# The last batch's down product in seven half-size products instead of eight

## The chip, the cores and the metric

The kernel runs on one core of a Trainium2 chip. A core has a matrix engine (PE, TensorE), a vector engine (DVE, VectorE), a scalar engine (ACT, ScalarE), a general engine (POOL, GpSimd) and a queue that issues transfers (SP, SyncE). Each engine works through its own list of instructions strictly in order, and waits at an instruction whose inputs, or whose room for the output, another engine has not yet released. The metric is the device time of one execution in microseconds (us), the median over several runs.

## The reference

The input is 8 batches of 512 rows of 512 numbers, all in 32-bit floats. Every row goes through an attention layer and then through a feed-forward layer; both are wrapped in the same way:

```
x = x + layernorm(attention(layernorm(x)))
x = x + layernorm(ffn(layernorm(x)))
```

The feed-forward layer, cut to what matters here:

```
x_up   = x @ W_up.T   * scale_up            # 512 -> 2048
x_gate = x @ W_gate.T * scale_gate
h = silu(x_gate) * x_up
h = hadamard(h * SU_dp) / 64                # folded into the weights by the kernel
y = h @ W_down.T * (Wscale_dp * 64)         # 2048 -> 512: the "down product"
```

For one batch the down product multiplies a 512 x 2048 matrix by a 2048 x 512 matrix and scales column j of the result by `Wscale_dp[j]`. After it comes the layer norm over each row of 512 numbers (mean and variance of the row), and the residual `x` is added.

## The kernel before, in words

The kernel first runs the attention of all batches, then the feed-forward layer. The feed-forward layer takes batches two at a time; the up and gate products of a pair are themselves computed by Strassen's scheme (`deep`, L1123 to L1144: small 128x256 products `d`, with sums on DVE, ACT and POOL around them). Each finished block of `h`, 128 of the 2048 inner values by 512 rows, is called `g` (written by DVE at L1160) and kept on chip. There are NI = 16 blocks per batch. Between the small products PE is given parts of the down product of earlier batches (`down_parts`, L1225): for a block `g` and each of the four groups of 128 rows (t = 0..3) one matrix product into the accumulator `psy` of that group, 512 columns wide. In 32-bit floats PE runs every matrix product as two passes, so the profile counts two MATMUL records for each.

At the end of a batch `finish` (L1245) empties the four accumulators: DVE multiplies by the output scale `wsdp_bc` (L1250), takes mean and variance (`bn`, L99 and L100), POOL makes the inverse deviation (`inverse_std`, L104 and L105), DVE the shift (`shift_of`, L114 for four groups at once or L112 for one), ACT applies both (L1272), POOL adds the residual (L1275) and SP sends the rows out (L1276). These steps are put off in a list `ends` and are taken from it by `proceed`.

The change concerns the last part of the program, the lines from `b = NB - 1` on. At that point batch 6 still lacks its last three blocks (12 products), and the whole down product of batch 7 is to be done. The 16 blocks of weights for batch 7 lie on chip in four tiles `wd_home` (names `xb` and `wdl` in the trace); the last eight of them are loaded by SP just before (L1093). The order is written out by hand:

- `down_rows` on group 0 of batch 7, inner blocks 0 to 13 (14 products, L1516),
- the 12 remaining products of batch 6 (`down`), then all of `ends` for batch 6 (`proceed`),
- inner blocks 14 and 15 of group 0, then loads of the four residual tiles (L1544),
- for each further group its 16 products first, and then `end_rows` of the group before it. `end_rows` is: DVE scale (L1522), mean and variance (L99, L100), POOL inverse deviation (L104, L105), DVE shift (L112), ACT (L1527), residual add on POOL, or for the last group on DVE (L1528), and the output transfer (L1529).

The accumulators of this part come from `ubank`, a pool of four PSUM banks used in turn: the fifth tile that is asked for can be written only when the first has been read. Side tiles come from `pr_tile` (six of two rows of 512).

Of the kernel before, what the change touches and what calls it, by code (L numbers as in the profile page):

```python
# [10 lines left out]
F32 = mybir.dt.float32  # L11
BF16 = mybir.dt.bfloat16
I32 = mybir.dt.int32
AF = mybir.ActivationFunctionType
ALU = mybir.AluOpType
AX = mybir.AxisListType

P = 128
# [3 lines left out]
NT = S // P  # L22
INTER = 2048
NI = INTER // P
# [9 lines left out]
def sandwich_kernel(  # L34
# [19 lines left out]
    nc = tc.nc  # L54
# [6 lines left out]
    stat = ctx.enter_context(tc.tile_pool(name="stat", bufs=12))  # L61
# [13 lines left out]
    wsdp_bc = const.tile([P, D], F32, name="wsdp_bc")  # L75
# [21 lines left out]
    def bn(dst, src, name):  # L97
        st = stat.tile([P, 6], F32, tag="st", name=f"st_{name}")
        nc.vector.bn_stats(out=st, in_=src)  # L99
        nc.vector.bn_aggr(out=dst, in_=st)  # L100

    def inverse_std(mv, n, name):
        rs = stat.tile([P, NT], F32, tag="rs", name=f"rs_{name}")
        nc.gpsimd.tensor_add(rs[:, :n], mv[:, :n, 1], eps[:, :n])  # L104
        nc.gpsimd.tensor_tensor(rs[:, :n], rs[:, :n], nhalf[:, :n], ALU.pow)  # L105
        return rs

    def shift_of(mv, rs, n, name):

        sh = stat.tile([P, NT], F32, tag="sh", name=f"sh_{name}")  # L110
        if n == 1:
            nc.vector.tensor_scalar(sh[:, 0:1], mv[:, 0, 0:1], rs[:, 0:1], -1.0, ALU.mult, ALU.mult)  # L112
            return sh
        nc.vector.scalar_tensor_tensor(  # L114
            sh[:, :n], mv[:, :n, 0], -1.0, rs[:, :n], ALU.mult, ALU.mult
        )
        return sh
# [4 lines left out]
    NH = NI // 2  # L122
# [31 lines left out]
    rows = [(b, t) for b in range(NB) for t in range(NT)]  # L154
    room = {}
    xrow, xflat, xb = {}, {}, {}
# [63 lines left out]
    ops, home = {}, []  # L220
# [21 lines left out]
    with ExitStack() as actx:  # L242
# [474 lines left out]
        for t in range(NT):  # L717
            xn[0, t] = row.tile([P, D], F32, tag="xn", name=f"xn_0_{t}", bufs=3)
            rs, sh = norm0[t]
# [139 lines left out]
        for t in range(NG * NT):  # L859
            n, c = divmod(t, NT)  # L860
            b, i = divmod(t, NK * NT)
# [73 lines left out]
        b = NB - 1  # L935
# [24 lines left out]
        for qc in range(NT):  # L960
            y, rs, sh = ys.pop((b, qc))
# [16 lines left out]
    def ubank(name):  # L978
        return ps_u.tile([P, S], F32, tag="u", name=name)
# [8 lines left out]
    HS = S // 2  # L988
# [8 lines left out]
    def pr_tile(name):  # L997
        return fs.tile([P, 2, S], F32, tag="pr", name=name, bufs=6)
# [72 lines left out]
    def order_of(b):  # L1071
        return [f for i in range(NH) for f in ((i, i + NH) if b % 2 == 0 else (i + NH, i))]
# [10 lines left out]
    wd_last = []  # L1083
# [11 lines left out]
    wd_home = []  # L1095
# [53 lines left out]
    waiting = {b: [] for b in range(NB)}  # L1149
# [136 lines left out]
    def proceed(by=None):  # L1286
        if ends and by in (None, ends[0][0]):
            ends.pop(0)[1]()
# [3 lines left out]
    def part():  # L1292
        if not queue:
            queue.extend(down_parts())
        if queue:
            queue.pop(0)()
# [210 lines left out]
        scale(b, f, c[:, 1], c[:, 0])  # L1507


    b = NB - 1  # L1510
    blocks = [g for _, g, _, _ in waiting[b]]
    assert order_of(b) == [f for f, _, _, _ in waiting[b]]

    def down_rows(ps, t, lo, hi):
        for n in range(lo, hi):
            nc.tensor.matmul(  # L1516
                ps, lhsT=blocks[n][:, ts(t, P)], rhs=wd_last[n], start=n == 0, stop=n == NI - 1
            )

    def end_rows(ps, t, eng):  # L1520
        y = pr_tile(f"fy_{b}_{t}")[:, 0]
        nc.vector.tensor_mul(y, ps, wsdp_bc)  # L1522
        mv = stat.tile([P, NT, 2], F32, tag="mvf", name=f"mvz_{t}")
        bn(mv[:, 0, :], y, f"z{t}")
        rs = inverse_std(mv, 1, f"z{t}")
        sh = shift_of(mv, rs, 1, f"z{t}")
        nc.scalar.activation(y, y, AF.Identity, bias=sh[:, 0:1], scale=rs[:, 0:1])  # L1527
        eng.tensor_add(y, rest[t], y)  # L1528
        nc.sync.dma_start(out=out[b, ts(t, P), :], in_=y)  # L1529

    now[0] += 2
    while queue:
        part()
    ps = ubank("psz_0")
    down_rows(ps, 0, 0, NI - 2)
    while turn_of[0] < b:
        down()
    while ends:
        proceed()
    down_rows(ps, 0, NI - 2, NI)  # L1540
    rest = []
    for t in range(NT):
        rest.append(fs.tile([P, D], F32, tag="sig", name=f"xres_{b}_{t}", bufs=4))
        nc.sync.dma_start(out=rest[t], in_=x1d[b][ts(t, P), :])  # L1544
    for t in range(NT):
        if t + 1 < NT:
            following = ubank(f"psz_{t + 1}")
            down_rows(following, t + 1, 0, NI)
        end_rows(ps, t, nc.vector if t == NT - 1 else nc.gpsimd)
        ps = following  # L1550


def _rope_table():
# [61 lines left out]
```

## Time and profile before

| | us |
|---|---|
| median of 3 runs | 2101.75 (2101.75, 2101.75, 2103.98) |
| the profiled execution's own time | 2102.66 |
| its span, first to last instruction | 2100.9 |
| PE busy over the span | 2076.8 (99%) |
| POOL busy over the span | 1575.4 (75%) |
| DVE busy over the span | 1414.4 (67%) |
| ACT busy over the span | 745.3 (35%) |
| granted TensorE clock, mean over the span | 0.999 |

In the profile `out<-in` names what an instruction writes and reads, with buffer numbers left out; all times are us from the start of the span unless they are durations. An `x16` behind a row says that it merges 16 records of the same kind. PE records overlap (a pass ends after the next has begun), so the pace is read from starts. `PEld` is the load of a product's left operand, which runs beside PE. In brackets stands the idle time before an instruction and what ended it. The page has no line on the distance between the profiled execution's own time (2102.66) and the span (2100.9): 1.8 us lie outside the first and last instruction.

### The profile page before, as it was taken

What the parts mean: (1) busy time and instruction counts of PE and PEld (TensorE: products, weight loads), DVE (VectorE), ACT (ScalarE), POOL (GpSimd) and SP (SyncE); (2) the same over time, 40 slices, a digit from 0 to 9 for tenths busy, and PEclk for the clock granted to TensorE, in tenths of its full rate; (3) what the DMA queues carried; (4) which work ended last, traced back from release to release, by engine and by line L of the source; (5) the groups of instructions that cost most, each with busy time, mean ns of one, the idle gap of its engine ahead of it and who ended that gap; (6) DMA issues with size and microseconds to landing.
All of it is one profiled execution on the core that took longest, in us unless ns stands there. A gap on an engine that the chain in (4) does not pass through costs nothing.

```text
span 2100.9 us, 26741 instructions
## 1 busy us (share of the span) xinstructions
PE 2076.8 (99%) x9035; PEld 1057.4 (50%) x9042; DVE 1414.4 (67%) x2356; ACT 745.3 (35%) x1199; POOL 1575.4 (75%) x1629
## 2 busy tenths in 40 slices
PE   8999999999999999999999999999999999999998
PEld 4333333333333333344444677676676766777753
DVE  5698777676767677465545866678866678656542
ACT  3554545555555545522121122222222222222211
POOL 4787979787878889645453678788888879787852
PEclk9999999999999999999999999999999999999999
DMA  3112121212121122237454444444343344444432
GB/s 122 37 31 51 42 54 49 47 51 52 46 57 46 32 66 72 70 104 221 145 166 152 146 143 148 133 138 149 130 157 131 131 137 144 138 158 136 138 112 70
DMA packets 215913, 218.12 MB, mean 104 GB/s; under 512 B 87376, under 2 KB 147920, under 8 KB 215776
## 3 DMA queue, kind: packets, MB, share of 16 engines
q1 hardware_dynamic: 215424, 215.32, 33.2%
q8 instruction: 72, 1.18, 0.2%
q0 software_dynamic: 352, 1.08, 0.1%
q14 instruction: 65, 0.53, 0.1%
HBM read 169.18 MB, written 46.92 MB: 103 GB/s over the span
## 4 chain that ended last, share of the span: by engine, by line
PE 94%; DVE 3%; issue 1%; POOL 1%; ACT 1%; DMA 0%; SPq 0%; POOLq 0%; DVEq 0%; ACTq 0%
PE d L1123 24%; PE psy L1225 18%; PE s L527 6%; PE ops L606 6%; PE ps_k L439 5%; PE ps_y L662 5%; PE t L573 5%; PE u L1106 5%; PE g L1106 4%; PE psz L1516 3%; PE t L564 3%; PE l L623 2%; PE ps_q L454 2%; PE ps_v L466 1%; PE ps_cq L407 1%; PE fxh L207 1%
## 5 line engine op out<-in xcount | busy, mean ns | idle before, releaser
L1225 PE MATMUL psy<-wd,g 128*128 128x512 f32 x896 | 448.9, 592 | 0.0
L535 DVE TENSOR_REDUCE nm<-s 128x2 f32<-128x1024 f32 x256 | 300.8, 1216 | 175.1 <-PE s L527 175.1
L1347 POOL TENSOR_TENSOR pr<-pr,pr 128x512 f32<-128x512 f32 x294 | 391.6, 1357 | 9.0
L594 POOL TENSOR_TENSOR p<-p,p 128x512 f32<-128x512 f32 x244 | 330.2, 1384 | 22.1 <-PE ops L606 22.1
L585 ACT ACTIVATE p<-t 128x1024 f32<-128x1024 f32 x256 | 251.8, 1023 | 89.0 <-PE t L573 89.0
L1123 PE MATMUL d<-xb,wq 128*128 128x256 f32 x992 | 254.2, 380 | 1.9 <-DVE inner L1139 1.4
L1123 PEld LDWEIGHTS d<-tt,wq 128*128 128x128 f32 x864 | 164.0, 190 | 144.4 <-issue 106.0
L1123 PE MATMUL d<-tt,wq 128*128 128x256 f32 x864 | 233.8, 379 | 0.2 <-DVE pr L1144 0.2
L1140 POOL TENSOR_TENSOR pr<-inner 128x256 f32<-128x256 f32 x168 | 126.0, 750 | 138.5 <-DVE inner L1139 105.9
L1123 PEld LDWEIGHTS d<-xb,wq 128*128 128x128 f32 x992 | 186.7, 190 | 62.4 <-issue 30.1
L1225 PEld LDWEIGHTS psy<-wd,g 128*128 128x128 f32 x896 | 169.7, 190 | 49.3 <-issue 29.4
L1136 ACT COPY inner<-d 128x256 f32<-128x256 f32 x168 | 62.6, 373 | 309.6 <-PE d L1123 291.5
L1132 ACT COPY inner<-d 128x256 f32<-128x256 f32 x168 | 62.6, 372 | 300.3 <-PE d L1123 193.2
L527 PE MATMUL s<-kT,qT 32*128 32x512 f32 x1024 | 153.8, 639 | 0.7 <-DVE nm L535 0.7
L573 PE MATMUL t<-qT,kT 32*128 32x512 f32 x1024 | 142.8, 598 | 0.0
L606 PE MATMUL ops<-p,v 128*32 128x512 f32 x1024 | 136.8, 605 | 0.0
L1142 POOL TENSOR_TENSOR pr<-pr,inner 128x256 f32<-128x256 f32 x168 | 136.5, 813 | 0.0
L1123 PE MATMUL d<-T,wq 128*128 128x256 f32 x496 | 127.6, 380 | 0.2
L1144 DVE TENSOR_TENSOR pr<-d,inner 128x256 f32<-128x256 f32 x168 | 70.5, 420 | 75.5 <-PE d L1123 72.9
L439 PE MATMUL ps_k<-xT,wkr_sb 128*128 128x512 f32 x256 | 118.3, 605 | 0.7 <-ACT xT L397 0.7
L662 PE MATMUL ps_y<-wo_sb,oT 128*128 128x512 f32 x256 | 115.8, 593 | 0.9 <-DVE oT L657 0.6
L1135 DVE TENSOR_TENSOR inner<-d,inner 128x256 f32<-128x256 f32 x168 | 70.5, 419 | 62.4 <-PE d L1123 62.0
(219 smaller groups left out, 3263.8 us busy)
## 6 DMA issues: line engine op xcount, KB each, us to landing
wq<-wdeep SPq DMA_DIRECT2D x168, 448.0 KB, 4.2
wd<-wdd SPq DMA_DIRECT2D x112, 256.0 KB, 2.8
wdeep<-w SPq DMA_DIRECT2D x32, 448.0 KB, 5.5
xr<-in_x SPq DMA_DIRECT2D x32, 256.0 KB, 2.8
xin<-x1d SPq DMA_DIRECT2D x32, 256.0 KB, 4.0
xres<-x1d SPq DMA_DIRECT2D x32, 256.0 KB, 3.3
out<-fy SPq DMA_DIRECT2D x32, 256.0 KB, 2.0
rec<-rd SPq DMA_DIRECT2D x124, 64.0 KB, 2.0
```

Of the source, the lines that this page charges most:

```text
L439: nc.tensor.matmul(ps, lhsT=wkr_sb[:, k, ts(g, P)], rhs=xT[b][:, k, :], start=(k == 0), stop=(k == NK - 1),)
L527: nc.tensor.matmul(sp[j // 2][:, j % 2, :], lhsT=qT[b][rows, g, ts(qc, P)], rhs=kT[b][rows, g, :], start=True, stop=True,)
L535: nc.vector.tensor_reduce(nms[n][:, qc, 2 * h : 2 * h + 2], sp[h], AX.X, ALU.max, negate=True)
L573: nc.tensor.matmul(sp[j // 2][:, j % 2, :], lhsT=kT[b][rows, g, ts(c, P)], rhs=qT[b][rows, g, :], start=False, stop=True,)
L585: nc.scalar.activation(pt[n, c, h], sp[h], AF.Exp)
L594: nc.gpsimd.tensor_add(into, into, pt[n, c, j // 2][:, j % 2, :])
L606: nc.tensor.matmul(o_ps[n][j * DH : (j + 1) * DH, :], lhsT=vv[b][:, c, ds(g * P + j * DH, DH)], rhs=pt[n, c, j // 2][:, j % 2, :], start=( ...
L662: nc.tensor.matmul(ps, lhsT=oT[b][:, k, ts(qc, P)], rhs=wo_sb[:, k, :], start=False, stop=(k == NK - 1),)
L1106: nc.tensor.matmul(ps, lhsT=w[:, SLOT[n], k, :], rhs=rhs[:, k, :], start=k == 0, stop=k == 1)
L1123: nc.tensor.matmul(ps, lhsT=w[:, INNER[m]], rhs=rhs[m], start=True, stop=True)
L1225: nc.tensor.matmul(ys_[t], lhsT=g[:, ts(t, P)], rhs=w, start=n == 0, stop=n == NI - 1)
L1347: nc.gpsimd.tensor_add(pr[n][:, h], pr[a][:, h], pr[b][:, h])
```

## The change

The down product of batch 7 is cut into halves in all three directions: rows (256 + 256), inner values (blocks 0 to 7 and 8 to 15) and columns (256 + 256). Strassen's scheme in Winograd's form gets the four result quarters from seven products of halves instead of eight, with sums of operands before the products and sums of results after them. A product of halves is 2 groups of 128 rows x 8 inner blocks = 16 matrix products that are 256 columns wide.

- Products 1, 2 and 4 have one PSUM bank for each group of 128 rows; products 5, 6, 7 and 3 have both groups in one bank.
- `sums_of(5)`, `(6)`, `(7)`, `(3)` make sums of `g` blocks on POOL (8 instructions of 128x256 each); `sums_of(5)`, `(6)`, `(7)`, `(4)` make sums of weights on DVE (4 instructions of 128x512 each). `sums_of(3)` and `(4)` also multiply the output scale into weights on DVE (8 instructions of 128x256 each).
- The first half of products 1 and 2 stands where the 14 products of group 0 stood; their second half comes after the 12 products of batch 6.
- `sums_of(5)`, `(6)` and `(7)` are issued ahead of the remaining products and the `ends` of batch 6, so they stand ahead of these on DVE's and POOL's lists. The copies of product 1 (`m1`) stand behind the `ends` on ACT's list.
- The sums of the results go over ACT (copies), DVE and POOL; the output scale is put in where the terms lie.
- Each output row of 512 is closed in two parts: statistics of its left and right 256 columns are taken apart and aggregated; DVE multiplies by the inverse deviation and adds the residual in one instruction, ACT adds the shift, and each half goes out in a transfer of its own (8 instead of 4).

The engines' lists change only behind this point: PE gets 112 products 256 wide in place of 64 products 512 wide, POOL 52 instructions in place of 17, DVE 76 in place of 30, ACT 15 in place of 8, SP 8 output transfers in place of 4 (all counted from the first instruction after the last `g` block).

The diff, cut to its core:

```diff
-    def down_rows(ps, t, lo, hi):
-        for n in range(lo, hi):
-            nc.tensor.matmul(
-                ps, lhsT=blocks[n][:, ts(t, P)], rhs=wd_last[n], start=n == 0, stop=n == NI - 1
-            )
...
     now[0] += 2
     while queue:
         part()
-    ps = ubank("psz_0")
-    down_rows(ps, 0, 0, NI - 2)
...
+    def sums_of(n):
+        if n in (5, 6, 7, 3):
+            for i in range(NH):
+                if n == 5:
+                    nc.gpsimd.tensor_add(sum1[:, i], A[7](i), A[4](i))
+                elif n == 6:
+                    nc.gpsimd.tensor_sub(sum2[:, i], sum1[:, i], A[1](i))
+                elif n == 7:
+                    nc.gpsimd.tensor_sub(A[7](i), A[1](i), A[7](i))
+                else:
+                    nc.gpsimd.tensor_sub(A[3](i), A[2](i), sum2[:, i])
+        for j in range(NT):
...
+            if n == 5:
+                nc.vector.tensor_sub(ws1[:, two], b12, b11)
+            elif n == 6:
+                nc.vector.tensor_sub(ws2[:, two], b22, ws1[:, two])
+            elif n == 7:
+                nc.vector.tensor_sub(b12, b22, b12)
+            elif n == 3:
+                for i in range(2):
+                    nc.vector.tensor_mul(b22[:, i], b22[:, i], wsdp_bc[:, HS:])
+            elif n == 4:
+                nc.vector.tensor_sub(b21, b21, ws2[:, two])
+                for i in range(2):
+                    nc.vector.tensor_mul(b21[:, i], b21[:, i], wsdp_bc[:, :HS])
...
+    def last_product(n, rows=(0, 1), lo=0, hi=NH):
+        for r in rows:
+            if (n, r) not in acc:
+                ps = ubank(f"psz_{n}_{r}").rearrange("p (r s) -> p r s", r=2)
+                if n in (1, 2, 4):
+                    acc[n, r] = ps[:, 0]
+                else:
+                    acc[n] = ps
+                    acc[n, 0], acc[n, 1] = ps[:, 0], ps[:, 1]
+            for i in range(lo, hi):
+                nc.tensor.matmul(
+                    acc[n, r], lhsT=A[n](i)[:, ts(r, P)], rhs=W[n](i), start=i == 0, stop=i == NH - 1
+                )
...
+    for n in (1, 2):
+        last_product(n, hi=NH // 2)
+    for n in (5, 6, 7):
+        sums_of(n)
     while turn_of[0] < b:
         down()
     while ends:
         proceed()
-    down_rows(ps, 0, NI - 2, NI)
+    for n in (1, 2):
+        last_product(n, lo=NH // 2)
...
+    def close_rows(t):
+        h, r = divmod(t, 2)
+        mv, rs = of_rows.pop(t)
+        sh = shift_of(mv, rs, 1, f"z{t}")
+        for half in (left, right):
+            cols = ts(half is right, HS)
+            o = half[h][:, r]
+            nc.vector.scalar_tensor_tensor(o, o, rs[:, 0:1], rest[t][:, cols], ALU.mult, ALU.add)
+            nc.scalar.activation(o, o, AF.Identity, bias=sh[:, 0:1])
+            nc.sync.dma_start(out=out[b, ts(t, P), cols], in_=o)
+
+    for r in range(2):
+        nc.scalar.copy(m1[:, r], acc[1, r])
+        nc.vector.tensor_add(left[0][:, r], acc[2, r], m1[:, r])
+    for r in range(2):
+        nc.vector.tensor_mul(left[0][:, r], left[0][:, r], wsdp_bc[:, :HS])
+        rows_stats(r, 0, left[0][:, r])
+    last_product(5)
+    nc.scalar.copy(m5, acc[5])
+    sums_of(3)
+    last_product(6)
+    nc.vector.tensor_add(u2, acc[6], m1)
+    nc.gpsimd.tensor_add(v, u2, m5)
+    for r in range(2):
+        nc.gpsimd.tensor_mul(v[:, r], v[:, r], wsdp_bc[:, HS:])
+    sums_of(4)
+    last_product(7)
+    nc.vector.tensor_add(u3, acc[7], u2)
+    nc.gpsimd.tensor_add(right[1], u3, m5)
+    for r in range(2):
+        nc.vector.tensor_mul(u3w[:, r], u3[:, r], wsdp_bc[:, :HS])
+        nc.gpsimd.tensor_mul(right[1][:, r], right[1][:, r], wsdp_bc[:, HS:])
+        rows_stats(r + 2, 1, right[1][:, r])
+    last_product(3)
+    nc.vector.tensor_add(right[0], acc[3], v)
+    for t in range(2):
+        rows_stats(t, 1, right[0][:, t])
+        head_rows(t)
+    for t in range(2):
+        close_rows(t)
+    for r in range(2):
+        last_product(4, rows=(r,))
+        nc.vector.tensor_add(left[1][:, r], acc[4, r], u3w[:, r])
+        rows_stats(r + 2, 0, left[1][:, r])
+        head_rows(r + 2)
+    for r in range(2):
+        close_rows(r + 2)
```

## The prediction

> **What bounds the kernel now.** I read the page's first part, then the chain of waits over the last 75 us (the change touches nothing before 2027 us), then the timeline there, then the granted clock by stretches.
>
> ```profile
> PE 2076.8 (99%) x9035; PEld 1057.4 (50%) x9042; DVE 1414.4 (67%) x2356; ACT 745.3 (35%) x1199; POOL 1575.4 (75%) x1629
> ```
>
> ```profile
> 2024.07 1.73 PE d L1123 x8
> ...
> 2027.94 12.02 PE psz L1516 x28
> 2039.96 10.30 PE psy L1225 x24
> 2050.26 42.93 PE psz L1516 x100
> 2093.19 0.02 issue
> 2093.21 0.70 DVE fy L1522
> ```
>
> PE is busy 99%, and from 2027.94 to 2093.19 the chain holds nothing but PE: 152 passes without a gap. After its last pass come 7.71 us of closing work to the span's end (2100.9 - 2093.19). A 512-column pass is paced at 42.93/100 = 0.4293 us, a 256-column pass at 1.73/8 = 0.2158.
>
> The timeline shows what waits cost the engines that the change loads (start, duration, instruction):
>
> ```profile
> 1946.16 0.73 POOL L1140 TENSOR_TENSOR pr<-inner 128x256 f32<-128x256 f32 x1 [0.47 <-DVE inner L1139]
> 1946.85 0.73 POOL L1142 TENSOR_TENSOR pr<-pr,inner 128x256 f32<-128x256 f32 x1
> ...
> 2027.46 2.85 DVE L1160 SCALAR_TENSOR_TENSOR g<-pr,wsu 128x512 f32<-128x512 f32 x2
> ...
> 2028.58 1.19 POOL L1140 TENSOR_TENSOR pr<-inner 128x256 f32<-128x256 f32 x1
> ...
> 2029.73 1.17 POOL L1142 TENSOR_TENSOR pr<-pr,inner 128x256 f32<-128x256 f32 x1
> ...
> 2030.97 2.49 POOL L1347 TENSOR_TENSOR pr<-pr,pr 128x512 f32<-128x512 f32 x2
> ...
> 2033.50 0.75 DVE L1160 SCALAR_TENSOR_TENSOR g<-pr,wsu 128x512 f32<-128x512 f32 x1 [3.19 <-POOL pr L1347]
> ...
> 2054.55 1.02 POOL L105 TENSOR_TENSOR rs_o<-rs_o,nhalf 128x4 f32<-128x4 f32 x1
> ...
> 2055.80 2.93 ACT L1272 ACTIVATE fy<-fy,sh_o,rs_o 128x512 f32<-128x512 f32 x4 [22.81 <-DVE sh_o L114]
> ```
>
> A 128x256 sum on POOL takes 0.73 and follows the one before after 0.69 when DVE is quiet. When DVE runs an operation with two inputs from SBUF beside it, both slow down: POOL's two sums end at 2029.77 and 2030.90, 1.13 apart, and the two DVE operations take 2.85 instead of twice 0.75. So a pair (one DVE sum of 512, one POOL sum of 256) costs 1.13, as if they took turns.
>
> ```profile
> 2093.20:2095.70 2.50, 0.00 (x0) 0.00 (x0) 1.57 (x3) 0.00 (x0) 0.69 (x2) 1.00 0.00 0
> 2095.90:2100.90 5.00, 0.00 (x0) 0.00 (x0) 0.78 (x2) 0.81 (x1) 0.00 (x0) 0.50 0.14 54
> ```
>
> ```profile
> 1.51 5.06 PE L284 MATMUL busy<-wsdp_bc 128*128 128x128 f32 x22 [1.51 <-DVE wsdp_bc L279]
> ...
> 7.09 0.61 PE L284 MATMUL busy<-wsdp_bc 128*128 128x128 f32 x4
> ```
>
> In the first block the third column from the end is the granted clock: from 2.7 us after the last pass it is 0.50. The second block shows a cold start: 22 passes of 128 columns take 5.06 us (0.22 apart), the same passes from 7.09 on are 0.11 apart. So PE ran at half pace for about 5.4 us.
>
> **The change part by part.**
>
> *Fewer columns on PE.* Removed: 64 products x 2 passes x 0.4293 = 54.95 us. Added: 112 x 2 x 0.2158 = 48.34. Gain 6.61 us if PE never waits. The 24 `psy` passes stay.
>
> *PE up to product 5.* From 2027.78 (start of the first pass): 64 passes of products 1 and 2 x 0.2158 = 13.81 and 24 x 0.4293 = 10.30, so PE asks for product 5 at 2051.9. Weights are no obstacle: SP's issues before the tail are unmoved, and before, blocks of these loads were read at 2034.6.
>
> *Product 5 needs a bank.* It takes the bank of product 1's first rows, which ACT must have copied (L1639). On ACT that copy stands behind the four L1272 of batch 6; these wait for DVE's shift (L114), it for POOL's L104 and L105, and on POOL those stand behind all 24 sums of `sums_of(5)`, `(6)`, `(7)`. Before, POOL was idle there for 20.8 us; the cover was PE's own work, since nothing of PE's waited for batch 6's closing.
>
> POOL: the first sum starts at 2033.42. Beside it DVE has L1160 and 12 weight sums, all with two inputs from SBUF: 13 pairs. I take turns at 1.13 (the row above): sum 13 ends at about 2047.8, sum 14 at 2048.9, and ten more at 0.69 end at 2055.8. Bounds: no interference at all, 24 x 0.69, end 2049.9; fully one after the other, 0.68 (a free 512 sum) + 0.73 = 1.41 a pair, end about 2059.3. I stay with 1.13, measured on the same shapes.
>
> [...]
>
> DVE's 12 sums end at 2048.3, the four L1250 and statistics (as before, 0.6 and 0.8 apart) at about 2054.1, so POOL is the later. Then, as at 2054 to 2060 before: L104 0.15, L105 1.10, 0.23 to ACT's start, L1272 2.93, copy 0.27: product 5 starts at 2055.8 + 4.7 = 2060.5. PE has waited 8.6 us. Everything of PE's stands behind that wait.
>
> *PE after it.* Products 5, 6, 7, 3, 4: 160 passes x 0.2158 = 34.53, and 0.16 to the end of the last: 2095.2, against 2093.19: **+2.0**. I looked for further waits. Product 7 needs POOL's last sums (2055.8). Product 3 starts 20.7 us after product 5; its operand comes from 8 more POOL sums behind the four L1275, of which two wait for residual transfers issued after the first two outputs, as before (3.3 us): done near 2072.5, 8 us early. Product 4's weights (12 DVE operations after product 6, sharing turns with 3 of POOL's) are done about 8 us after product 6, and are wanted 13.8 us after it. No wait in any.
>
> *The clock.* PE is idle for over 8 us, and the row at 2095.90 shows half clock 2.7 us after the last pass. Half pace loses half of its own duration. At the start it lasted 5.4 us, a loss of 2.7; if the clock can rise as quickly as it fell (2.7 us at most), the loss is 1.35. I take **+2.2**, nearer to the start, which is the same step. Zero would need the clock to hold through 8 us, against that row.
>
> [...]
>
> *The end.* Before: 4.74 us from the last pass to the last output issue (2097.93), then 2.97. After: DVE add of 256 (0.42), statistics 0.44, aggregate 0.21, POOL 0.9 beside DVE's shift and first two closing operations, then shift and two operations of the last rows (0.21 and 0.8 with one turn lost), ACT 0.6, issue: about 4.4. The transfer and what follows I leave at 2.97 (half the bytes; bounds -0.5 and +0.3 for four issues close together at 0.4 each). Together **-0.35**. The residual add moved from POOL to DVE and the eight outputs (SP, 0.34 each) hide beside products 3 and 4, except the last.
>
> *Sum.* +2.0 + 2.2 - 0.35 = **+3.85** on the profiled execution's 2102.66, so 2106.5. That execution lay 0.9 above the median; on the median the forecast is **2105.6 us**, +0.18%.
>
> **The rivals.**
>
> A. [...] The restart is as slow as the start of the program, or slower: loss 2.7 or more, sum +4.35 or more, 2106.1. It decides from a loss of 2.55 on, since 4.2 us is 0.2%. For it: the only rise that the trace shows. Against it: one case, and the fall was quicker.
>
> B. *POOL and DVE fully exclude each other: slower.* A pair costs 1.41: product 5 starts 3.5 us later, sum +7.35, 2109.1. It decides from a pair of 1.16 on. Against it: the two ends 1.13 apart.
>
> C. *The clock holds.* +1.65, 2103.4. Against it: the 0.50 row.
>
> D. *POOL and DVE do not meet.* POOL done at 2049.9, then the same chain of 4.7: product 5 at 2054.6, a wait of 2.8 us; PE ends 3.8 earlier, end -0.35: -4.1, 2097.6. Against it: the rows at 2027 to 2031.
>
> E. *The change does what its count says.* No wait at all: -6.61 - 0.35, 2094.8. Against it: four ACT operations alone stand between batch 6's statistics and the copy.
>
> **How the numbers follow.** Forecast 43%, A 22%, B 18%, C 9%, D 6%, E 2%. 0.2% (4.2 us) is about what a measurement of this kernel can tell from no change: its three runs lie 2.2 us apart. The forecast, C and half of D fall within it, A and B slower, the other half of D and E faster: faster 0.05, within 0.55, slower 0.40. The range, 2100.5 to 2109.0, holds the forecast, A, C and nearly all of B (pairs up to 1.40); it leaves out D and E and the corner where turns and clock are both at their worst.
>
> **What would show it.** PE idle ahead of `psz` (L1583) once, from about 2052 to 2060, released by ACT (L1639), and no other gap over 0.5 us; POOL's L1545, L1547 and L1549 near 1.1 apart for the first 13 and 0.69 after; DVE's L1556 to L1560 at about 1.1 instead of 0.68; a granted clock of 0.5 for 2 to 7 us after the restart; after PE's last pass about 7.3 us. I am wrong if POOL keeps 0.69 beside DVE (D), if the clock stays at 1.00 (C), or if products 3 or 4 wait too.

## The result, and the profile after

The changed kernel takes **2105.6 us** (median of 17 runs, 2103.85 to 2108.41) against 2101.75 us (median of 17 runs, 2101.11 to 2103.98). The ratio is 1.0017, 95% interval 1.0010 to 1.0025: slower by 0.1 to 0.25%. That is little, but 1 lies outside the interval. The profiled execution of the changed kernel took 2104.33 us (span 2102.6), 1.3 below its median; that of the kernel before lay 0.9 above its own. The two traces alone therefore differ by only 1.7 us, and below each part is compared by itself.

The share of busy time hardly moved (the page's first part; each entry is busy time, share, instructions):

```profile
PE 2072.7 (99%) x9138; PEld 1077.0 (51%) x9138; DVE 1442.9 (69%) x2406; ACT 746.2 (35%) x1206; POOL 1606.3 (76%) x1664
```

PE is still busy 99%, 4.1 us less than before. (DVE's count rose by 50, so its list behind the change holds 80 instructions, not the 76 given above.) The timeline of PE shows where the rest is (start, duration, instruction; in brackets the idle time before it):

```profile
2026.58 7.07 PE L1583 MATMUL psz<-xb,g 128*128 128x256 f32 x32
2033.48 10.46 PE L1225 MATMUL psy<-wd,g 128*128 128x512 f32 x24
2043.78 7.07 PE L1583 MATMUL psz<-wdl,g 128*128 128x256 f32 x32
2059.27 15.57 PE L1583 MATMUL psz<-T,xb 128*128 128x256 f32 x64 [8.42 <-issue]
...
2093.67 1.89 PE L1583 MATMUL psz<-wdl,g 128*128 128x256 f32 x8
```

Products 1 and 2 and batch 6 follow each other without a gap. Ahead of product 5 PE is idle for 8.42 us, once, and nowhere else. The bracket counts from the modelled end of the pass before; counted from starts, product 5 comes 8.6 us later than the pace would have it (2059.27, where 2043.78 + 32 x 0.2158 = 2050.69). The first 64 passes behind it then take 15.57 us where 64 x 0.2158 + 0.16 = 13.97 would do. From the first pass of `psz` to the end of the last it is 68.98 us (2095.56 - 2026.58), against 65.40 before: +3.58. The releaser is given as "issue", so this view doesn't say what product 5 waited for.

The timelines of POOL and of ACT in the same stretch:

```profile
2032.22 8.65 POOL L1545 TENSOR_TENSOR xb<-g,g 128x256 f32<-128x256 f32 x8
2040.83 8.21 POOL L1547 TENSOR_TENSOR xb<-xb,g 128x256 f32<-128x256 f32 x8
2049.01 5.49 POOL L1549 TENSOR_TENSOR g<-g 128x256 f32<-128x256 f32 x8
2054.46 0.20 POOL L104 TENSOR_TENSOR rs_o<-mvo,eps 128x4 f32<-128x4 f32 x1
```

```profile
2055.99 2.93 ACT L1272 ACTIVATE fy<-fy,sh_o,rs_o 128x512 f32<-128x512 f32 x4 [24.20 <-DVE sh_o L114]
2058.82 0.62 ACT L1639 COPY z_m<-psz 128x256 f32<-128x256 f32 x2
```

POOL's third group of eight sums takes 5.49 us; the first two, mostly beside DVE's weight sums, 8.65 and 8.21. DVE isn't quiet beside the third group. It runs batch 6's scale and statistics until 2052.67:

```profile
2047.00 2.47 DVE L1250 TENSOR_TENSOR fy<-psy,wsdp_bc 128x512 f32<-128x512 f32 x4
2049.40 0.68 DVE L99 BATCH_NORM_STATS2 st_o<-fy 128x6 f32<-128x512 f32 x1
```

These have one input in SBUF (`psy` lies in PSUM), and POOL keeps its 0.69 beside them.

Behind the sums come POOL's L104 and L105 (to 2055.76), DVE's shift, ACT's four L1272, and the copies; product 5 starts 0.1 us after the first copy has ended (2059.17). That is the chain of the forecast, in its order.

The granted clock by stretches (start:end, length, PE busy, then the clock; the last two columns are transfers):

```profile
2054.00:2055.00 1.00, 0.00 (x0) 1.00 0.00 0
2055.00:2056.00 1.00, 0.00 (x0) 0.76 0.00 0
2056.00:2062.00 6.00, 2.73 (x7) 0.50 0.39 128
2062.00:2063.00 1.00, 1.00 (x5) 0.82 0.76 285
```

A mean of 0.76 in 2055 to 2056 puts the fall at 2055.52, and 0.82 in 2062 to 2063 puts the rise at 2062.36: half clock for 6.84 us, 3.1 of them after PE's restart. Seven passes run at half pace there.

The end is shorter. SP's last issues, before and after:

```profile
2097.93 0.33 SPq L1529 DMA_DIRECT2D out<-fy  x1
```

```profile
2097.83 2.19 SPq L1636 DMA_DIRECT2D out<-fy  x4
```

From PE's last pass to the end of the last issue it was 2098.26 - 2093.19 = 5.07 us and is 2100.02 - 2095.56 = 4.46; from there to the span's end 2.64 and 2.58. The whole end, from PE's last pass to the end of the span, went from 7.7 to 7.0.

### The profile page after: what moved, and what is told of

Read it like the earlier page. It is cut to its first block, busy times and chain, and to the rows that moved or that the text cites. A ratio compares the mean times of both kernels' runs of the same rounds, so it can differ in the third digit from the quotient of the medians.

```text
span 2102.6 us, 27066 instructions
## 1 busy us (share of the span) xinstructions
PE 2072.7 (99%) x9138; PEld 1077.0 (51%) x9138; DVE 1442.9 (69%) x2406; ACT 746.2 (35%) x1206; POOL 1606.3 (76%) x1664
## 4 chain that ended last, share of the span: by engine, by line
PE 92%; DVE 3%; POOL 2%; issue 1%; ACT 1%; DMA 0%; POOLq 0%; SPq 0%; DVEq 0%; ACTq 0%
PE d L1123 23%; PE psy L1225 17%; PE s L527 6%; PE ops L606 6%; PE ps_k L439 5%; PE ps_y L662 5%; PE t L573 5%; PE u L1106 5%; PE g L1106 4%; PE t L564 3%; PE psz L1583 2%; PE l L623 2%; PE ps_q L454 2%; PE ps_v L466 1%; PE ps_cq L407 1%; PE fxh L207 1%
```

## The experiments

All start from the changed kernel. Two measures are used beside the time: the **work**, from PE's first pass of `psz` to the end of its last, and the **end**, from there to the end of the span. "Half" is the time at half clock after a restart inside the work. The work, the idle time, the half clock and the end are read from one profiled execution of each kernel; the six kernels whose closing is neither changed nor late have ends of 6.98 to 6.99 us, so 0.2 us in the end is a difference.

| kernel | median us (runs) | work | PE idle in it | half | end |
|---|---|---|---|---|---|
| before | 2101.75 (17) | 65.4 | 0 | 0 | 7.7 |
| changed | 2105.60 (17) | 69.0 | 8.4 | 3.1 | 7.0 |
| e1_bank_each | 2104.38 (11) | 68.4 | 4.7 | in the waits | 7.0 |
| e2_copies_first | 2095.78 (6) | 58.8 | 0 | 0 | 7.6 |
| e1c_bank_each_rows | 2096.40 (10) | 59.3 | 0.2 | 0 | 8.3 |
| e3_sums7_later | 2098.87 (11) | 61.8 | 2.7 | 0 | 7.0 |
| e8_no_weight_sums | 2099.00 (10) | 63.6 | 3.1 | 3.0 | 7.0 |
| e4_passes_in_wait | 2110.11 (5) | 74.4 (15.5 idle passes) | 0 | 0 | 7.0 |
| e5_fewer_passes | 2103.13 (10) | 67.5 (7.8 idle passes) | 0.7 | 0 | 7.0 |
| e9_one_part | 2106.51 (1) | 70.0 | 8.5 | 5.0 | 7.2 |
| e10_scale_behind | 2106.49 (1) | 70.4 | 8.4 | 6.0 | 7.4 |
| e7_all_moves | 2098.29 (11) | 60.8 | 1.7 | 0 | 8.4 |
| e6_sums4_earlier | 2097.03 (1) | 58.8 | 0 | 0 | 7.3 |
| e11_less_load | 2095.24 (5) | 58.8 | 0 | 0 | 7.5 |

### What does product 5 wait for?

My theory: a bank, which ACT frees late only because the copy of product 1 stands behind batch 6's closing. The rival: its operands, the sums of POOL and DVE.

**Product 1's copies moved ahead on ACT** (e2_copies_first):

```diff
-    while ends:
-        proceed()
     for n in (1, 2):
         last_product(n, lo=NH // 2)
+    m1, m5 = room_for("z_m")
+    for r in range(2):
+        nc.scalar.copy(m1[:, r], acc[1, r])
+    while ends:
+        proceed()
...
-    m1, m5 = room_for("z_m")
...
     for r in range(2):
-        nc.scalar.copy(m1[:, r], acc[1, r])
```

> Banks as in the changed kernel, but on ACT the two copies of product 1 (L1639) are issued ahead of batch 6's closing, so that they stand before the four L1272. POOL's 24 sums and DVE's 12 stay where they are. My theory (of the chain POOL, DVE L114, ACT L1272, ACT L1639 it is only the place in ACT's order that couples product 5 to POOL): the copies run as soon as product 1 has ended, about 2 to 3 us before product 5 is asked for; no gap, clock 1.00, about 2094.5, the same as with a bank for each product. Rival (POOL's and DVE's sums are late as operands, or DVE's addition of product 2 behind L114 holds product 7): a gap remains ahead of product 5 or 7, above 2097.

Measured: 2095.78 us, ratio to the kernel before 0.9969 (0.9958 to 0.9981). ACT copies at 2046.79 and 2048.52, each as its rows are done, and product 5 starts with no gap. PE's timeline of this kernel:

```profile
2044.87 7.07 PE L1583 MATMUL psz<-wdl,g 128*128 128x256 f32 x32
2051.77 13.98 PE L1583 MATMUL psz<-T,xb 128*128 128x256 f32 x64
```

The 64 passes take 13.98 us, full pace. POOL's last sum still ends only at 2055.64, and the four L1272 start behind it:

```profile
2057.12 2.93 ACT L1272 ACTIVATE fy<-fy,sh_o,rs_o 128x512 f32<-128x512 f32 x4 [8.23 <-DVE sh_o L114]
```

The sums are neither fewer nor earlier, and PE waits for nothing. The rival falls. The time misses the 2094.5 by 1.3 us; the work is as expected (58.8), the end is 0.65 longer than in the changed kernel. That is taken up below.

**A bank each for products 1 and 2** (e1_bank_each). Two banks stay free, so product 5 needs no copy:

```diff
-                if n in (1, 2, 4):
+                if n == 4:
...
-    for n in (1, 2):
-        last_product(n, hi=NH // 2)
+    last_product(1)
...
-    for n in (1, 2):
-        last_product(n, lo=NH // 2)
+    last_product(2)
```

> Undone here: banks of their own for the row blocks of products 1 and 2. Each of the two products has one bank, as products 5, 6, 7 and 3 have; product 1 runs whole ahead of batch 6's last passes, product 2 whole behind them. Number of passes, sums on POOL and DVE, and the order on ACT stay. Products 5 and 6 then find the third and the fourth bank free. My theory (product 5 waited for a bank only): the idle stretch of 8.4 us ahead of product 5 goes, the clock stays at 1.00 up to the last pass, product 5's first pass follows the pass before at 0.22 us although POOL's last sum and the four L1272 end no sooner than before; product 7 takes product 1's bank at about 14 us after product 5 has started, 5 us after it was copied. PE from its first pass of psz to its last: 58.8 us (65.41 - 6.61) instead of 68.99. Time about 2094.5. Rival 1 (product 5 waited for its operands, the sums of POOL and DVE): the wait stays, 2105 to 2106. Rival 2 (the wait only moves to product 7 or 3): a gap of some us there, 2097 to 2102.

Measured: 2104.38 us. A miss by 10 us. The gap ahead of product 5 is gone, but there are others, in PE's timeline:

```profile
2034.58 1.22 PE L1583 MATMUL psz<-wdl,g 128*128 128x256 f32 x2 [2.95 <-DMA wdl<-wdd]
2037.29 2.51 PE L1583 MATMUL psz<-wdl,g 128*128 128x256 f32 x4 [1.50 <-DMA wdl<-wdd]
```

Running product 1 whole ahead of batch 6 needs blocks 4 to 7 of its weights, and they land from about 2034.6 to 2040. The changed kernel's halves, blocks 0 to 3 first, are what kept PE off them. PE waited 4.7 us in all, and the clock was 0.50 from 2034.2 to 2044.5, so that 16 passes ran at half pace. My edit had changed two things at once.

**The same with passes that need no late weights** (e1c_bank_each_rows): ahead of batch 6 only the first half of products 1 and 2 for the first 128 rows. The diff is against e1_bank_each.

```diff
-    last_product(1)
+    for n in (1, 2):
+        last_product(n, rows=(0,), hi=NH // 2)
...
-    last_product(2)
+    for n in (1, 2):
+        last_product(n, rows=(0,), lo=NH // 2)
+        last_product(n, rows=(1,))
```

> Again one bank for each of products 1 and 2, but with passes that need only the first four blocks of weights ahead of batch 6's last 24: of the first 128 rows, the first half of both products (16 passes). Behind batch 6's come the second half for those rows and then all of the second 128 rows (48 passes). ACT's order and all sums are those of the changed kernel. Theory (the first bank-for-each kernel lost its gain to weights that had not landed, and to the clock that fell in that wait): no gap now ahead of batch 6's passes, none ahead of product 5, clock 1.00 throughout; from the first pass of psz to the last 58.8 us; about 2095.8, as with the copies moved first. Rival (a product needs its operands: POOL's sums): a gap ahead of product 5 of 8 us, 2105. Rival 2 (batch 6's last g is not ready 3.5 us sooner): a gap of up to 3.5 us ahead of or within psy's 24 passes, 2096 to 2099.

Measured: 2096.40 us, work 59.3, one idle stretch of 0.23 us (for a weight block of batch 6); product 5 follows without a gap at 2051.09, while the copies of product 1, still behind the four L1272, come at 2058.76. (The end of 8.3 us: DVE starts the addition for the last rows 1.7 us after PE's last pass.) Two unlike edits, one to ACT's order and one to the banks, take the 8.4 us away, and each leaves POOL's sums and DVE's as they were. It was the bank, by way of ACT's order.

### What makes the wait as long as it is?

**The sums for product 7 behind batch 6's shift** (e3_sums7_later): eight sums fewer on POOL ahead of L104.

```diff
-    for n in (5, 6, 7):
+    for n in (5, 6):
         sums_of(n)
     while turn_of[0] < b:
         down()
+    for _ in range(NT + 1):
+        proceed()
+    sums_of(7)
     while ends:
         proceed()
```

> Banks and ACT's order as in the changed kernel; the 8 POOL sums and 4 DVE sums for product 7 are issued behind batch 6's statistics, inverse deviation and shift, ahead of its four L1272. My theory (the length of POOL's queue ahead of L104 sets the wait): POOL now has 16 sums there, done near 2047.2, and L104 then waits for DVE's last statistics, which come about 4.5 us sooner than before, near 2049.5 to 2050; the same 4.8 us later product 5 starts: a wait of 3 to 4 us instead of 8.4. That is less than the 4.7 us for which the clock held after PE's last pass, so it stays at 1.00. Time 2105.6 - 4.8 - 2.5 = about 2098. Rival 1 (POOL's place doesn't matter, the four L1272 or the residual transfers set the wait): still above 8 us, 2105. Rival 2 (the sums of product 7 become the next wait): a new gap ahead of product 7, time over 2100.

Measured: 2098.87 us (2097.41 to 2101.07), in the profiled execution (2097.77) idle 2.71 and clock 1.00:

```profile
2054.24 14.05 PE L1583 MATMUL psz<-T,xb 128*128 128x256 f32 x64 [2.71 <-POOL g L1549]
```

The releaser named there can't be it: none of POOL's L1549 ends within 0.1 us ahead of 2054.24, but ACT's first copy of product 1 does, at 2054.14. POOL starts L104 at 2048.90, after a wait for DVE's statistics, and product 5 starts 5.3 us later. So POOL's queue ahead of L104 set the length, until DVE's statistics took its place.

**DVE's weight sums for products 5, 6 and 7 left out** (e8_no_weight_sums):

```diff
...
-            if n == 5:
-                nc.vector.tensor_sub(ws1[:, two], b12, b11)
-            elif n == 6:
-                nc.vector.tensor_sub(ws2[:, two], b22, ws1[:, two])
-            elif n == 7:
-                nc.vector.tensor_sub(b12, b22, b12)
-            elif n == 3:
+            if n == 3:
...
```

> The changed kernel without DVE's 12 weight sums for products 5, 6 and 7 (products 5 and 6 take other weights that lie there, product 4's sum takes another operand; the result is not the reference's). POOL's 24 sums and everything else stay. Theory (POOL's sums are slow because DVE's sums take turns with them): one pair at 1.13 remains, beside DVE's last L1160, the others follow each other at 0.69, so POOL is done about 5.3 us sooner, near 2049.2 where it was 2054.5; DVE's statistics are done near 2049.3 too, since its queue is shorter; product 5 starts 4.8 us later, near 2054.1, a wait of 3.3 us; the clock holds; 2105.6 - 5.1 - 2.6 = about 2098. Rival 1 (POOL's 1.13 is its own, from the tiles it reads): sums stay 1.13 apart, the wait stays 8.4, 2105.6. Rival 2 (full exclusion, 0.68 + 0.73 a pair): contradicted already if the spacing with DVE is 1.13.

Measured: 2099.00 us. POOL's timeline, to be laid beside that of the changed kernel:

```profile
2032.18 5.94 POOL L1545 TENSOR_TENSOR xb<-g,g 128x256 f32<-128x256 f32 x8
...
2043.55 5.52 POOL L1549 TENSOR_TENSOR g<-g 128x256 f32<-128x256 f32 x8
2049.04 0.19 POOL L104 TENSOR_TENSOR rs_o<-mvo,eps 128x4 f32<-128x4 f32 x1
```

The same 24 sums end 5.4 us sooner (2049.07 for 2054.50), DVE's statistics too, and the wait falls to 3.07 us. The turns of POOL and DVE are worth 5.4 us of the 8.4. But the clock did not hold, though I had expected it to for a wait this short. It fell at 2053.52 and rose at 2056.92; PE's timeline at the wait, then the clock:

```profile
2053.89 3.46 PE L1577 MATMUL psz<-xb,xb 128*128 128x256 f32 x8 [3.07 <-ACT z_m L1633]
```

```profile
2053.00:2054.00 1.00, 0.12 (x1) 0.76 0.42 160
2054.00:2056.00 2.00, 2.00 (x5) 0.50 0.75 217
2056.00:2057.00 1.00, 1.00 (x4) 0.54 0.96 348
```

### What does the clock cost?

**Passes in the wait** (e4_passes_in_wait), into a bank that batch 6 has left; each such product makes two passes, which the edit left out of account:

```diff
+    idle = ps_y.tile([P, D], F32, tag="y0", name="psidle")
+    for i in range(36):
+        nc.tensor.matmul(
+            idle[:, :HS], lhsT=A[1](i % NH)[:, :P], rhs=W[1](i % NH), start=i == 0, stop=i == 35
+        )
     last_product(5)
```

> The changed kernel with 36 more passes of 256 columns just ahead of product 5, into a bank of psy that batch 6 has left; nobody reads them. By the pace of 0.2158 us they take 7.8 us, inside the wait of 8.4 us, which otherwise stays. My theory (the wait costs twice: once as idle time, and once as the clock that falls in it): the granted clock stays at 1.00, the 160 passes from product 5 on take 34.7 us instead of 36.3, an idle rest of under 1 us remains, and the time falls by the loss of clock alone, 1.6 to 2.7 us: 2103 to 2104. Rival (the slow passes after the wait come from something else than idleness, the sums of POOL and DVE or the closing of batch 6 that run beside them): the seven passes 0.43 apart are still there, 2105.6.

Measured: 2110.11 us. The chain of waits of this kernel:

```profile
2045.65 6.91 PE psz L1583 x32
2052.56 15.54 PE psidle L1646 x72
2068.10 34.55 PE psz L1583 x160
```

72 passes put product 5 off by 15.5 us instead of 8.6, 7.0 more. Without these 7.0 the time would be 2103.1, 2.5 below the changed kernel. The 160 passes behind them take 34.55 us (34.70 from the first start to the last end), where the changed kernel's take 36.30, and none of them is slow.

**Half as many** (e5_fewer_passes; `range(18)`):

> The passes in the wait again, with half as many products: 18 products of 256 columns, and each makes two passes (the 36 products of the kernel before made 72 passes, 15.5 us, and outlasted the wait by 7.1 us). 36 passes x 0.2158 = 7.77 us inside the wait of 8.4. Theory (idleness costs the clock): product 5 starts when it did, 4.8 us after POOL's last sum; its 160 passes take 34.6 us; time lower than the changed kernel's by the loss of clock alone. The kernel with 72 passes gives 2105.6 + 7.1 - 2110.1 = 2.6 us for it, the profiled execution of the changed kernel 36.3 - 34.6 = 1.7: 2103.0 to 2103.9. Rival (the slow passes have another cause): 2105.6.

Measured: 2103.13 us (2102.38 to 2105.36), 2.5 below the changed kernel. PE is idle for 0.70 us ahead of product 5, and here the releaser has its name:

```profile
2059.54 14.05 PE L1583 MATMUL psz<-T,xb 128*128 128x256 f32 x64 [0.70 <-ACT z_m L1639]
```

The loss of clock is 2.5 us on the medians. They come from different sets of runs: set against the kernel before that was measured with each (2101.75 and 2102.04), it is 2.8, and the kernel with the copies moved gives 1.9 (2105.60 - 2095.78 = 9.8, plus the 0.65 by which its end is longer, less the 8.6 of the wait). So the cost on the median is 2 to 3 us and not known more closely. In single executions it depends on when the rise comes. At full clock the 160 passes behind a gap take 34.77 us from the first start to the last end (e3_sums7_later, e5_fewer_passes). By this they lost 1.5 us in the profiled execution of the changed kernel (36.29), 2.5 and 3.0 in the two kernels that follow (37.26 and 37.74), whose half clock lasted 10.2 us instead of 6.8. That of the first of them, the closing in one part:

```profile
2055.00:2056.00 1.00, 0.00 (x0) 0.51 0.00 0
2056.00:2065.00 9.00, 4.77 (x11) 0.50 0.34 117
2065.00:2066.00 1.00, 1.00 (x5) 0.87 0.00 0
```

### What does the closing give?

**In one part** (e9_one_part): each 128 rows with one operation on DVE, one on ACT and one output.

```diff
-        for half in (left, right):
-            cols = ts(half is right, HS)
-            o = half[h][:, r]
-            nc.vector.scalar_tensor_tensor(o, o, rs[:, 0:1], rest[t][:, cols], ALU.mult, ALU.add)
+        o = y[h][:, r]
+        nc.vector.scalar_tensor_tensor(o, o, rs[:, 0:1], rest[t], ALU.mult, ALU.add)
...
```

> The changed kernel with its closing of each 128 rows in one part: one DVE operation, one ACT operation and one output of 512 columns instead of two each of 256. PE and its wait stay as in the changed kernel. Theory (two parts overlap DVE with ACT): DVE 0.75 + ACT 0.80 in sequence instead of 0.39 + 0.48 + 0.51, and one issue instead of two: from PE's last pass to the end 7.1 to 7.3 us instead of 7.0, +0.2. Rival (the number of issues or the bytes behind the last one set the end): shorter than 7.0 by an issue of 0.4, or longer by more than 0.5.

Measured: end 7.24 against 7.0 us, one execution. Two parts are worth 0.25 us.

**Scale behind the additions** (e10_scale_behind): the operations on weights go, and four of 128x256 come, among them

```diff
-        nc.vector.tensor_add(left[1][:, r], acc[4, r], u3w[:, r])
+        nc.vector.tensor_add(left[1][:, r], acc[4, r], u3[:, r])
+        nc.vector.tensor_mul(left[1][:, r], left[1][:, r], wsdp_bc[:, :HS])
```

> The changed kernel with the output scale of products 3 and 4 applied behind the additions instead of inside the sums: 16 operations on weights go from DVE, 2 from POOL and 2 more from DVE, and 4 of 128x256 come, one of them between the last addition and its statistics. PE and its wait for product 5 stay. Theory: from PE's last pass to the end 7.0 + 0.35 = 7.35 us; the wait of 8.4 us and its clock as in the changed kernel. Rival (DVE's load at the end counts in the changed kernel too): 7.0 or less.

Measured: end 7.44 us, one execution. The scale inside the sums is worth 0.45 us. (Both kernels' times, one run each, lie above the changed kernel's median; their passes lost 2.5 and 3.0 us to the clock.)

### What is late once the wait is gone?

With the copies moved, the end took 7.64 us: DVE starts the addition for the last rows at 2087.51, 1.0 us after PE's last pass (2086.47). The chain of waits of that kernel (e2_copies_first) leaves PE at 2065.8:

```profile
2045.03 20.73 PE psz L1583 x96
...
2065.79 0.69 DVE z_u L1649
...
2067.11 1.70 DVE xb L1567 x2
```

DVE's 12 operations for product 4's weights take from 2066.4 to 2077.9: an L1567 takes 0.85 us here. Four L1563 of the same shape took 1.41 us in the changed kernel (2061.45) with POOL idle beside them. Here POOL is at its sums for product 3; in e11_less_load, where its list is the same up to them, they start at 2065.94. Product 7's result, ready at 2072.7, is read at 2077.9.

**Everything moved** (e7_all_moves). Beside the copies: the shift of batch 6 ahead of `sums_of(7)`, then two closings, `sums_of(3)`, `sums_of(4)`, the other closings; and the rows 256 to 383 are closed ahead of the addition for the last rows:

```diff
         head_rows(r + 2)
-    for r in range(2):
         close_rows(r + 2)
```

> Product 1's copies on ACT ahead of batch 6's closing (as before), and three more moves to relieve POOL and DVE at the end: batch 6's statistics and shift ahead of the sums of product 7; two of its four closings, then the sums for products 3 and 4, then the other two closings (so that POOL does not wait for the residual transfers ahead of product 3's sums, and product 4's weights are ready before POOL starts on it); rows 256 to 383 closed ahead of the addition for rows 384 to 511. With the copies moved alone, DVE was late for the last rows (its addition of the last product started 1.0 us after PE's last pass) and the end took 7.6 us. Theory (DVE's queue sets that end): DVE is idle and waiting when PE's last pass ends, the end takes 6.5 to 7.0 us, PE without a gap 58.8 us from its first pass of psz: 0.6 to 1.1 us less than with the copies alone, 2094.7 to 2095.2. Rival (the moves make product 7 or 3 wait for their sums): a gap on PE, over 2096.

Measured: 2098.29 us; the rival's gap, and a longer end. On DVE the additions of product 2, which free product 7's bank, now stood behind all those sums:

```profile
2074.10 1.96 PE L1583 MATMUL psz<-xb,g 128*128 128x256 f32 x8 [1.72 <-DVE fy L1648]
```

The end took 8.4 us: DVE adds the last rows at 2089.94, 1.8 us after PE's last pass (2088.15), because the shift of the rows before stands ahead of it and waits 0.93 us for POOL's inverse deviation.

**Product 4's sums earlier, nothing taken away** (e6_sums4_earlier; `sums_of(4)` moved ahead of the addition of product 6):

> Copies of product 1 moved ahead on ACT, and the sums for product 4 ahead of the addition of product 6, nothing taken away. Theory (load): DVE's 12 operations and POOL's closing of batch 6 and sums for product 3 still take turns, DVE is late for the last rows as with the copies alone, the end after PE's last pass takes 7.4 us or more. Rival (order alone): DVE is free when PE's last pass ends, 7.0 us. PE has no gap in both: 58.8 us from its first pass of psz; one look, about 2095 to 2096.

Measured: end 7.26 us, between the two expectations, in a single run; the addition for the last rows starts 0.66 us after PE's last pass. Order helps a little.

**Less to do** (e11_less_load): as the one before, product 3's scale behind its addition, and the rows before the last closed first.

```diff
...
             elif n == 3:
-                for i in range(2):
-                    nc.vector.tensor_mul(b22[:, i], b22[:, i], wsdp_bc[:, HS:])
+                pass
...
-    for r in range(2):
-        nc.gpsimd.tensor_mul(v[:, r], v[:, r], wsdp_bc[:, HS:])
...
```

> Copies of product 1 moved ahead on ACT, and then: the output scale of product 3 behind its addition (2 DVE operations of 256 instead of 8 on the weights and 2 of POOL's), the sums for product 4 ahead of the addition of product 6, and rows 256 to 383 closed ahead of the addition for rows 384 to 511. Theory (once product 5 starts on time, DVE and POOL with their turns have too much to do before product 4 ends; it is the load that must go): DVE's sums for product 4 then run while POOL waits for the residual transfers, POOL's eight sums for product 3 run without DVE beside them at 0.69, both are idle and waiting when PE's last pass ends. From there to the end 6.6 us (7.0 less the two closing operations of the rows before, which no longer stand in that chain); PE without a gap; from the first pass of psz to the end 65.4 us instead of 66.4 with the copies alone: about 2094.8. Rival (DVE stalls on POOL's inverse deviation of the rows 256 to 383 and is late for the last addition): end 7.5 us or more, 2096.

Measured: 2095.24 us, ratio 0.9964 (0.9950 to 0.9977). The load did go: DVE is idle ahead of product 3's result from 2077.19 to 2078.88. But the end is 7.5 us, the rival's. The chain of waits shows DVE between two waits for POOL's inverse deviation:

```profile
2083.83 0.34 DVE fy L1668
...
2084.95 0.20 POOL rs_z L104
...
2085.22 0.56 POOL rs_z L105
...
2085.80 0.21 DVE sh_z L112
2086.02 0.79 DVE fy L1635 x2
2086.80 0.35 DVE fy L1668
```

PE's last pass ends at 2085.78; DVE, which waits in order for the shift of the rows before, adds at 2086.72. This kernel and the one with the copies alone are not told apart (ranges 2094.21 to 2095.35 and 2094.95 to 2096.6), and both beat the kernel before by 6 us or more. The two halves of the last edit taken singly were not run.

## Why the prediction came out as it did

The forecast was 2105.6 on the median, and the median is 2105.6. That is closer than its terms deserve:

- **Fewer columns, -6.61:** right. Where nothing waits the work is 58.81 us for 65.40, -6.59.
- **Product 5 waits for a bank, 8.6 us:** right in place, releaser and size (product 5 came 8.6 us late, 8.42 by the bracket). Two edits, one to the banks and one to ACT's order ahead of the copy, remove it.
- **Pairs of POOL and DVE at 1.13 us, 0.69 without DVE:** right, and 13 pairs, as forecast: 13 of POOL's sums took about 1.17 us each, the first of all and the last ten about 0.73. Leaving DVE's side out ends POOL 5.4 us sooner. "When DVE is quiet" was too narrow: POOL also kept 0.69 beside DVE's scale and statistics. The full exclusion of rival B (1.41) and the undisturbed sums of rival D are out: the first eight sums took 8.65 us, one free and seven beside DVE, these 1.13 us apart: turns, at less than the 1.41 of both in sequence.
- **POOL to product 5, 4.7 us:** right (4.77).
- **The clock, +2.2:** right in kind: it fell to 0.50 in the wait (2055.52), and the seven passes from 2059.30 to 2062.30 took 3.00 us, 0.43 each. The size is 1.9 to 2.8 us on the medians, 1.5 in the profiled execution and 3.0 in the worst one seen, which is beyond my upper bound of 2.7. I had taken one fixed duration from the start of the program; it differs between executions (3.1, 5.0 and 6.0 us after the restart). That start was read from passes alone: the trace's record of the clock begins only at 6.87 us, and its column shows 1.00 before. Rival C (the clock holds) is out; rival A's condition, a loss of 2.55 or more, is met in one profiled execution and nearly in another, and for the median it can't be told from the forecast.
- **No other wait on PE:** right for this kernel. But the spare time in it (8 us for product 3's operand) was a gift of the wait itself: with product 5 on time, DVE was 1 us late for the last rows. Rival E's 2094.8 left that out; the kernels without the wait reached 2095.2 to 2096.4.
- **The end, -0.35:** too little; it is -0.7. What I took for the engines from the last pass on, 4.4 us, measured about 4.1 (issues end at 4.46, each 0.38); the transfer did stay the same.

Without the clock the terms measured add up to -6.6 + 8.6 - 0.7 = +1.3; the measured +3.85 leaves 2.5 for the clock, inside its 1.9 to 2.8. By that, a clock about 0.3 too cheap and an end 0.3 too dear cancelled in the forecast. The hit to a tenth is luck: single executions of the changed kernel lie 4.6 us apart, and the clock's cost is not known to better than 1 us. (In the working 1.73/8 is 0.2163, not 0.2158; over 224 passes that is 0.1 us, and the 0.2158 was the pace seen later, 34.55/160 = 0.2159.)

## What to carry to other kernels

When one engine is busy 99% of the time, a change that takes columns from it has to be followed on all the others: trace the first instruction that needs a bank or a buffer back to whoever frees it, through every queue in its order. Here 8.4 us plus the clock were lost to two copies of 0.4 us that stood behind unrelated work on an engine 35% busy, and moving those copies ahead turned a change of +0.2% into one of -0.3%. Idle stretches of 8.4 and 3.07 us on PE were paid for twice here, one of 2.71 was not; and spare time read from a trace with a wait in it is spare only as long as the wait is there.

## What the runs showed of the hardware that I had not expected

- **Half clock came in whole steps.** The stretches at 0.50 lasted 3.40 us (e8_no_weight_sums), 6.83 us (the changed kernel) and 10.24 us (e9_one_part, e10_scale_behind): one, two and three times 3.413, as closely as the rows can be read. In the changed kernel's trace the record of the clock begins at 7.53 us and has changes at 2055.52, 2062.35 and 2099.90: 2048.00, 6.83 and 37.55 us apart, which is 600, 2 and 11 times 3.413 (37.55/11, to 0.001). In the kernel before it begins at 6.87 and the clock falls at 2095.83, 612 such steps later. The fall did not come at one fixed time after the last pass: 2.6 us in the kernel before (2093.20), 2.7 in e8_no_weight_sums (2050.8), 4.7 in the wait of the changed kernel (2050.85). A wait of 2.71 us (e3_sums7_later) left the clock at 1.00, one of 3.07 us (e8_no_weight_sums) did not; what decides it was not shown.
- **Half clock came early in one program too, in code that no edit touches.** In the profiled execution of e6_sums4_earlier the clock was 0.50 from 30.00 to 33.30 us. In the changed kernel's it was 1.00 there, with as much work on PE ahead of it (3.26 us of passes from 25 to 29 us in both). The cause stays open. The first line is the changed kernel, the second, in its own block, e6_sums4_earlier:

```profile
30.00:33.30 3.30, 3.30 (x14) 1.00 0.00 0
```

```profile
30.00:33.30 3.30, 3.30 (x5) 0.50 0.00 0
```

PE reached its first pass of `psz` at 2026.51 us in e1c_bank_each_rows and at 2029.74 in e1_bank_each. So the parts here are compared from that pass on, and one run of this kernel says little below 2 us.
